# The inverse transform of a convolution in 32-column tiles, with the transpose on VectorE

## The chip, the cores and the metric

The kernel runs on one core of a Trainium2 chip. The metric is the device time in microseconds. Three runs of the kernel before gave 2071.14, 2072.65 and 2078.92 us; the median is 2072.65 us. All data is float32.

## The reference, cut to what matters

The program is a stack of two graph layers over 128 graphs of 128 nodes with 256 channels. The first layer normalizes x, and from the result h it makes a convolution over the nodes (1x1, then 17 taps, each with a batch norm), a message product over neighbours, and a gated update.

```
xc = transpose(h)                          # channels x nodes
c  = relu(bn1(conv1d(xc, conv1_w, 0)))
c  = bn2(conv1d(c, conv2_w, 8))            # 17 taps along the nodes
x_conv = transpose(relu(c + xc))
x_in = concat(x_conv, x_nmp)               # x_nmp: neighbours' messages
gi = x_in @ w_ih.T + b_ih ;  gh = h @ w_hh.T + b_hh
r = sigmoid(gi_r + gh_r) ;  z = sigmoid(gi_z + gh_z)
n = tanh(gi_n + r * gh_n)
x = x + (1 - z) * n + z * h
```

The second layer takes the first 25 nodes of each graph through five small graph convolutions and adds the result to x.

## The kernel before, in words

**The 17-tap convolution as products at frequencies.** The kernel doesn't run 17 products per node. It cuts the 128 nodes of a graph into two blocks of 64 outputs, each of which needs 80 inputs, and transforms these into F = 80 real frequency values. Stage A (`stage_a`) normalizes x, makes the 1x1 convolution and transforms into X. Stage B (`stage_b`) multiplies X by the transformed weights, frequency by frequency, and stores the result in DRAM as yd, with one 80x256 plane (frequency by channel) per block. Stage C (`stage_c`) reads four such planes at a time as the tile yt, transforms back with the constant matrix inv (80 frequencies by 64 nodes), and makes the gated update. A stage works on groups q of four graphs, so there are 32 groups.

**The start of stage C** is what the change touches. For each half of a group (two graphs), L703 makes two matmuls: inv is the stationary operand, with 64 columns, and the planes of block 0 or 1 of the two graphs are the moving operand, with 2 x 256 columns. They land in partitions 0 to 63 and 64 to 127 of the PSUM tile pi, so that pi holds nodes on partitions and channels along the free axis. ScalarE copies pi to xi in SBUF (L705). The rest of stage C wants channels on partitions. So the function turn_back (L710 to L724) transposes xi on TensorE, in blocks of 128x128, into the PSUM tile pc (L717); VectorE multiplies by the batch norm's scale and adds hT (the normalized input, channels on partitions), which gives xc (L720), and ScalarE adds the shift and applies Relu (L723). xc has two channel chunks (`xc[:, 0]` and `xc[:, 1]`) and two halves of columns.

**The gates** follow as products of weights with hT, xm (the neighbours' messages) and xc. They are made with a fast 2x2 scheme of seven products. For i below 3, product i takes a quarter of x as it stands; the others take one of four differences, which are made ahead on VectorE and are called th, tm and tc for the three inputs (`sums`, L586):

```
def factor(i, x, t):
    return ((x[:, 0, :D], x[:, 1, :D], x[:, 1, D:])[i] if i < 3
            else t[:, (3, 0, 1, 2)[i - 3]])
```

Products 0, 5 and 4 begin with the terms of hT and xm alone (the loop at L765, four matmuls each), and turn_back stands after the first of them. Then come the xc term of product 0 (L771), the sums tc (L773 to L775), three products of the hidden weights (L787 to L790, with VectorE's additions L791 and L792 behind them), all of product 1 (L794) and the xc terms of products 5 and 4, which read tc (L797, L802). At the end of a group GpSimd makes the update from r and z in two times three operations (L864, L865, L867); the result is transposed on TensorE as po (L884) while the next group already runs.

**What sets the order.** The kernel writes the order of its instructions by hand: each stage is a generator that issues some instructions and yields two numbers, the time that they are thought to take on TensorE and a pause. The class Order picks, by these numbers and by weights, which lane goes on. During stage C the lanes are the loads, stage C itself, the remaining message products (`early`), the normalization for the second layer (`rows`) and the second layer (`prepare`, `block`). Every engine then takes its instructions strictly in that order. PSUM tiles with the tag tmp rotate through five banks (`ptmp`), those with the tag gat through three (`pgat`). In SBUF, xi and tc share one buffer (tag tc), and xc has one buffer.

Of the kernel before, what the change touches and what calls it, by code (L numbers as in the profile page):

```python
# [9 lines left out]
FP = mybir.dt.float32  # L10
AF = mybir.ActivationFunctionType
ALU = mybir.AluOpType
# [3 lines left out]
B, N, D = 128, 128, 256  # L16
# [3 lines left out]
P = 128  # L20
GB = 4
NQ = B // GB

F = 80
# [17 lines left out]
WIDE = 32  # L42
# [165 lines left out]
def kernel(ctx: ExitStack, tc: tile.TileContext, x, adj, consts, vecs, w_se, conv1_w,  # L208
                    conv2_w, w_msg, b_msg, w_ih, w_hh, W1, W2, b2, fusion_w, out):
    nc = tc.nc  # L210
# [7 lines left out]
    ptmp = ctx.enter_context(tc.tile_pool(name="ptmp", bufs=5, space=PSUM))  # L218
# [14 lines left out]
    def c(name):  # L233
        a, b = CAT[name]
        return cst[:, a:b]
# [5 lines left out]
    ident = c("ident")  # L241
    fwd, inv = c("fwd"), c("inv")
# [15 lines left out]
    scl, sft = {}, {}  # L258
# [341 lines left out]
    def load_yt(q, h):  # L600

        if q < NQ:
            IN2[q, h] = LATE["co"].tile([F, GB, D], FP, tag="yt", name=f"yt{q}_{h}", bufs=2)
            x0 = (q % BQ * 2 + h) * GB
            nc.sync.dma_start(out=IN2[q, h],
                              in_=yd[q // BQ][x0:x0 + GB].rearrange("x f c -> f x c"))
# [80 lines left out]
    def stage_c(q):  # L687
# [7 lines left out]
            load_yt(q, 1)  # L695
            yield 0.0, 6.0
        fr = LATE["co"]
        xi = fr.tile([P, GB, D], FP, tag="tc", name=f"xi{q}")
        for h in range(2):
            yt = IN2.pop((q, h))  # L700
            pi = ptmp.tile([P, 2, D], FP, tag="tmp", name=f"pi{q}_{h}")
            for b in range(2):
                nc.tensor.matmul(pi[b * 64:(b + 1) * 64], inv[:F], yt[:, b::2],  # L703
                                 start=True, stop=True)
            nc.scalar.activation(xi[:, 2 * h:2 * h + 2], pi, AF.Copy)  # L705
            load_yt(q + 1, h)
            yield 0.86, 0.0
        xc = fr.tile([P, 2, 512], FP, tag="xc", name=f"xc{q}")

        def turn_back():  # L710

            for h in range(2):
                s = slice(h * D, (h + 1) * D)
                pc = ptmp.tile([P, 2, D], FP, tag="tmp", name=f"pc{q}_{h}")
                for co in range(2):
                    for i in range(2):
                        nc.tensor.transpose(pc[:, co, i * P:(i + 1) * P],  # L717
                                            xi[:, 2 * h + i, co * P:(co + 1) * P], ident)
                for co in range(2):
                    nc.vector.scalar_tensor_tensor(xc[:, co, s], pc[:, co],  # L720
                                                   scl["bn2"][:, co:co + 1], hT[:, co, s],
                                                   op0=ALU.mult, op1=ALU.add)
                    nc.scalar.activation(xc[:, co, s], xc[:, co, s], AF.Relu,  # L723
                                         bias=sft["bn2"][:, co:co + 1])  # L724

        wrz, wn, wh = LATE["wrz"], LATE["wn"], LATE["wh"]

# [5 lines left out]
        def part(ps, w, i, xs, first, last, again=False):  # L733


            n = [(m, o) for o in xs for m in range(w.shape[3] // P)]
            for j, (m, (k, x, t)) in enumerate(n):
                nc.tensor.matmul(ps[:, m], w[:, i, k, m * P:(m + 1) * P], factor(i, x, t),  # L738
                                 start=first and j == 0, stop=last and j == len(n) - 1,
                                 skip_group_check=again)  # L740
# [24 lines left out]
        for ps, i in ((p1, 0), (p6, 5), (p5, 4)):  # L765
            part(ps, wrz, i, early, True, False)
            yield 1.75, 0.0
            if i == 0:
                turn_back()
                yield 0.9, 0.0  # L770
        part(p1, wrz, 0, xs[2:], False, True)  # L771
        nc.scalar.activation(u2, p1, AF.Copy)  # L772
        tcs, todo = sums("tc", q, xc)  # L773
# [351 lines left out]
    for bat, (during_a, during_b) in enumerate(((0.66, 0.5), (0.2, 0.65))):  # L1125
# [12 lines left out]
        tc.tile_pool(name="co", bufs=1, side="right", reuse_waits="tile"))  # L1138
    loads = Lane([stage_n(q) for q in range(NQ)])
    groups = Lane([stage_c(q) for q in range(NQ)], ahead=2)  # L1140
    second = [setup_1()] + [part(blk) for blk in range(NBLK) for part in (prepare, block)]
    beside.weight = 0.5
# [43 lines left out]
```

## Time and profile before

| | |
|---|---|
| Median of three runs | 2072.65 us |
| Profiled execution, span of the core | 2070.6 us |
| TensorE busy | 2032.3 us (98%) |
| VectorE busy | 1161.9 us (56%) |
| ScalarE busy | 712.7 us (34%) |
| GpSimd busy | 730.1 us (35%) |
| mean granted TensorE clock | 0.993 |
| inverse transforms (L703) | 64 halves, first at 681.4 us, last at 1946.7 us |

PE is TensorE, PEld its weight loads, DVE VectorE, ACT ScalarE, POOL GpSimd, SP SyncE. The profile is of one execution; its span runs from the first to the last instruction. A matmul appears as two records and a transpose on TensorE as one. "L720" is line 720 of the kernel. In a row of the groups, "out<-in" names the tiles written and read, then come the shapes, the count, the busy time in us, the mean length of one in ns, and the time for which the engine was idle just before, with what ended it. The chain of work that ended last is followed back from the last instruction; on it, each piece begins when the one before it lets it begin. Lengths of neighbouring TensorE records overlap, because matmuls are pipelined; so the pace is read from the starts, or from the chain.

### The profile page before, as it was taken

How to read it: one execution, taken by the hardware profiler on the slowest of the kernel's cores; microseconds unless marked ns; L12 is line 12 of the kernel's file. 1: busy time of each engine (PE TensorE's matmuls, PEld its weight loads, DVE VectorE, ACT ScalarE, POOL GpSimd, SP SyncE). 2: the span in 40 equal slices, each digit the busy share in tenths (PEclk: the TensorE clock that was granted, in tenths of full speed). 3: DMA queues.
4: the chain of work that ended last, by engine and by line, in shares of the span. 5: the costliest groups of instructions: out<-in, count | busy, mean ns of one | idle time of the engine just before them, and what ended most of it. 6: DMA issues, size and time to landing. Idle time of an engine off the chain costs nothing.

```text
span 2070.6 us, 31082 instructions
## 1 busy us (share of the span) xinstructions
PE 2032.3 (98%) x11316; PEld 1649.4 (80%) x11316; DVE 1161.9 (56%) x2711; ACT 712.7 (34%) x1611; POOL 730.1 (35%) x898
## 2 busy tenths in 40 slices
PE   7998999999999999999999999999999999999998
PEld 5667888888888788788778787878787888778875
DVE  6774445874433556646654654566456655654542
ACT  4663223444222444233222332232332323323333
POOL 3552665333664123322422243233223323233230
PEclk9999999999999999899999999999999999999999
DMA  9997788545777444223323232322232332323121
GB/s 215 294 284 237 259 273 269 180 153 202 254 257 249 142 125 139 75 75 90 85 62 90 84 83 76 106 79 75 82 93 72 81 96 80 86 77 102 35 74 52
DMA packets 190135, 281.72 MB, mean 136 GB/s; under 512 B 23625, under 2 KB 143374, under 8 KB 189982
## 3 DMA queue, kind: packets, MB, share of 16 engines
q1 hardware_dynamic: 156942, 185.46, 31.4%
q0 software_dynamic: 32656, 93.98, 14.3%
q8 instruction: 90, 1.47, 0.3%
q14 instruction: 63, 0.52, 0.1%
q10 hardware_dynamic: 384, 0.28, 0.1%
HBM read 187.34 MB, written 92.27 MB: 135 GB/s over the span
## 4 chain that ended last, share of the span: by engine, by line
PE 93%; DVE 2%; DMA 2%; POOL 1%; issue 1%; ACT 1%; SPq 0%; DVEq 0%; POOLq 0%; ACTq 0%
PE p L738 42%; PE pa L526 7%; PE pm L630 5%; PE ph L1044 5%; PE pz L1053 5%; PE pc L421 4%; PE pb L526 3%; PE pi L703 3%; PE pf L432 3%; PE px L656 3%; PE pg L1087 2%; PE po L884 1%; PE pc L717 1%; PE pw L474 1%; PE ph L410 1%; PE py L1027 1%
## 5 line engine op out<-in xcount | busy, mean ns | idle before, releaser
L864 POOL TENSOR_TENSOR d<-hTc,r 128x512 f32<-128x512 f32 x64 | 81.9, 1280 | 244.4 <-ACT r L861 233.8
L526 PE MATMUL pa<-wf,X 128*128 128x256 f32 x640 | 152.2, 381 | 0.0
L893 POOL DMA_DIRECT2D out<-xt x128 | 72.0, 569 | 214.5 <-DVE xt L890 211.6
L558 DVE SCALAR_TENSOR_TENSOR y<-pa,kk 128x512 f32<-128x512 f32 x78 | 53.8, 690 | 151.2 <-ACT kk L557 151.1
L753 ACT ACTIVATE z<-z,brz 128x256 f32<-128x256 f32 x128 | 58.1, 501 | 226.7 <-DVE z L810 192.9
L738 PE MATMUL p<-th,wrz 128*128 128x256 f32 x512 | 132.8, 382 | 0.0
L738 PE MATMUL p<-tm,wrz 128*128 128x256 f32 x512 | 132.3, 381 | 0.0
L738 PE MATMUL p<-tc,wrz 128*128 128x256 f32 x512 | 131.5, 379 | 0.0
L526 PEld LDWEIGHTS pa<-wf,X 128*128 128x128 f32 x640 | 118.1, 190 | 16.2 <-issue 2.0
L630 PE MATMUL pm<-wmsg,hT 128*128 128x256 f32 x512 | 123.5, 387 | 0.0
L421 PE MATMUL pc<-c1w,hTa 128*128 128x256 f32 x512 | 121.6, 384 | 1.2 <-ACT hTa L412 1.2
L720 DVE SCALAR_TENSOR_TENSOR xc<-pc,s_bn,hTc 128x256 f32<-128x256 f32 x128 | 53.1, 478 | 123.3 <-PE pc L717 123.3
L1046 ACT ACTIVATE hh<-ph,vec 128x96 f32<-128x96 f32 (+3 forms) x160 | 64.2, 402 | 136.6 <-PE ph L1044 127.0
L630 PEld LDWEIGHTS pm<-wmsg,hT 128*128 128x128 f32 x512 | 97.1, 193 | 16.0 <-ACT kk L557 1.4
L1044 PE MATMUL ph<-yz,w 128*128 128x96 f32 (+3 forms) x640 | 108.4, 322 | 1.0 <-issue 1.0
L421 PEld LDWEIGHTS pc<-c1w,hTa 128*128 128x128 f32 x512 | 94.5, 191 | 18.3 <-DVE h L424 4.8
L738 PEld LDWEIGHTS p<-tm,wrz 128*128 128x128 f32 x512 | 97.9, 191 | 13.5
L1053 PE MATMUL pz<-hh,w 128*128 128x96 f32 (+3 forms) x640 | 107.3, 321 | 0.0
L738 PEld LDWEIGHTS p<-th,wrz 128*128 128x128 f32 x512 | 94.9, 191 | 13.0 <-issue 0.8
L738 PEld LDWEIGHTS p<-tc,wrz 128*128 128x128 f32 x512 | 95.0, 190 | 12.1 <-issue 0.5
L738 PE MATMUL p<-hTc,wrz 128*128 128x256 f32 x384 | 102.9, 391 | 1.6 <-ACT u L772 1.6
L1044 PEld LDWEIGHTS ph<-yz,w 128*128 128x128 f32 x640 | 86.7, 190 | 21.0 <-issue 15.4
(202 smaller groups left out, 4557.1 us busy)
## 6 DMA issues: line engine op xcount, KB each, us to landing
wf<-wfd SPq DMA_DIRECT2D x160, 256.0 KB, 3.5
wfd<-ws POOLq DMA_DIRECT2D x64, 320.0 KB, 9.2
yd<-y POOLq DMA_DIRECT2D x80, 256.0 KB, 4.3
yt<-yd SPq DMA_DIRECT2D x64, 320.0 KB, 5.0
w<-in_W SPq DMA_DIRECT2D x40, 512.0 KB, 3.6
xa<-in_x SPq DMA_DIRECT2D x128, 128.0 KB, 5.5
hTd<-hTa POOLq DMA_DIRECT2D x32, 512.0 KB, 6.6
hT<-hTd SPq DMA_DIRECT2D x32, 512.0 KB, 6.2
```

What stands on the lines that cost most here:

```text
L421: nc.tensor.matmul(pc[:, i], hT[:, k, (2 * h + i) * N:(2 * h + i + 1) * N], c1w[:, k], start=(k == 0), stop=(k == 1))
L432: nc.tensor.matmul(pf[:, i, :F * NB], h1[:, 2 * h + i, k * P:(k + 1) * P], fwd, start=True, stop=True)
L526: nc.tensor.matmul(ps, xk(k), WF[f][:, k, s], start=(k == 0), stop=(k == 1))
L630: nc.tensor.matmul(pm[:, i], hT[:, k, j * N:(j + 1) * N], LATE["wmsg"][:, k], start=(k == 0), stop=(k == 1))
L656: nc.tensor.matmul(px[:, dc, i], msgs[h][:, i, dc * P:(dc + 1) * P], aT[:, 2 * h + i], start=True, stop=True)
L703: nc.tensor.matmul(pi[b * 64:(b + 1) * 64], inv[:F], yt[:, b::2], start=True, stop=True)
L738: nc.tensor.matmul(ps[:, m], w[:, i, k, m * P:(m + 1) * P], factor(i, x, t), start=first and j == 0, stop=last and j == len(n) - 1, skip_g ...
L864: nc.gpsimd.tensor_sub(d, hT[:, dc], r[:, dc])
L893: nc.gpsimd.dma_start(out=out[q * GB + j, WIDE:].rearrange("(t n) c -> n t c", n=WIDE), in_=xt[j * WIDE:(j + 1) * WIDE, 1:4])
L1044: nc.tensor.matmul(ph, w1[:, k, m * P:(m + 1) * P], yz[:, k, :, o:o + n], start=(k == 0), stop=(k == 1))
L1046: nc.scalar.activation(hh[:, m], ph, AF.Relu, bias=v("b1", g * 4 + m))
L1053: nc.tensor.matmul(pz, w2[:, g, m, cc * P:(cc + 1) * P], hs[g][:, m], start=(m == 0), stop=(m == 3))
```

## The change

The inverse transform swaps nothing between stationary and moving, but cuts both finer. For each half group there are four blocks n of 32 nodes (two blocks of 64, each in two) and four slices w of 32 channels in each of the two chunks of 128. A matmul now has 32 columns of inv as the stationary operand, and slice w of both chunks and both graphs as the moving operand, 2 x 2 x 32 = 128 columns. It writes partitions 32w to 32w + 31 of pi, so that a quadrant of partitions stands for one channel slice, and a run of 32 values along the free axis is the slice's channels. VectorE's transpose of 32x32 blocks then turns each block on its way from PSUM to xi, which leaves channels on partitions and nodes along the free axis. The transposes on TensorE, the tile pc and the ScalarE copy are gone, and so is the step turn_back: the scale, the addition of hT and Relu follow each half's transpose at once, with xi in SBUF as input. Both halves are now one step of the generator, without a pause between them.

```diff
-        xi = fr.tile([P, GB, D], FP, tag="tc", name=f"xi{q}")
+        xi = fr.tile([P, 2, 512], FP, tag="tc", name=f"xi{q}")
+        xc = fr.tile([P, 2, 512], FP, tag="xc", name=f"xc{q}")
         for h in range(2):
             yt = IN2.pop((q, h))
-            pi = ptmp.tile([P, 2, D], FP, tag="tmp", name=f"pi{q}_{h}")
-            for b in range(2):
-                nc.tensor.matmul(pi[b * 64:(b + 1) * 64], inv[:F], yt[:, b::2],
-                                 start=True, stop=True)
-            nc.scalar.activation(xi[:, 2 * h:2 * h + 2], pi, AF.Copy)
+            pi = ptmp.tile([P, 2, 2, 4, WIDE], FP, tag="tmp", name=f"pi{q}_{h}")
+            for n in range(4):
+                o = n % 2 * WIDE
+                for w in range(4):
+                    nc.tensor.matmul(
+                        pi[w * WIDE:(w + 1) * WIDE, :, :, n].rearrange("p k g c -> p g k c"),
+                        inv[:F, o:o + WIDE],
+                        yt[:, n // 2::2].rearrange("f g (k w c) -> w f g k c", k=2, w=4)[w],
+                        start=True, stop=True)
+            nc.vector.transpose(xi[:, :, h * D:(h + 1) * D],
+                                pi.rearrange("p k g n c -> p k (g n c)"))
             load_yt(q + 1, h)
-            yield 0.86, 0.0
-        xc = fr.tile([P, 2, 512], FP, tag="xc", name=f"xc{q}")
-
-        def turn_back():
-
-            for h in range(2):
-                s = slice(h * D, (h + 1) * D)
-                pc = ptmp.tile([P, 2, D], FP, tag="tmp", name=f"pc{q}_{h}")
-                for co in range(2):
-                    for i in range(2):
-                        nc.tensor.transpose(pc[:, co, i * P:(i + 1) * P],
-                                            xi[:, 2 * h + i, co * P:(co + 1) * P], ident)
-                for co in range(2):
-                    nc.vector.scalar_tensor_tensor(xc[:, co, s], pc[:, co],
-                                                   scl["bn2"][:, co:co + 1], hT[:, co, s],
-                                                   op0=ALU.mult, op1=ALU.add)
-                    nc.scalar.activation(xc[:, co, s], xc[:, co, s], AF.Relu,
-                                         bias=sft["bn2"][:, co:co + 1])
+            s = slice(h * D, (h + 1) * D)
+            for co in range(2):
+                nc.vector.scalar_tensor_tensor(xc[:, co, s], xi[:, co, s],
+                                               scl["bn2"][:, co:co + 1], hT[:, co, s],
+                                               op0=ALU.mult, op1=ALU.add)
+                nc.scalar.activation(xc[:, co, s], xc[:, co, s], AF.Relu,
+                                     bias=sft["bn2"][:, co:co + 1])
+        yield 1.8, 0.0
...
         for ps, i in ((p1, 0), (p6, 5), (p5, 4)):
             part(ps, wrz, i, early, True, False)
             yield 1.75, 0.0
-            if i == 0:
-                turn_back()
-                yield 0.9, 0.0
```

## The prediction

> **What bounds the kernel now.** I began with the busy shares, the slices and the chain of work that ended last.
>
> ```profile
> PE 2032.3 (98%) x11316; PEld 1649.4 (80%) x11316; DVE 1161.9 (56%) x2711; ACT 712.7 (34%) x1611; POOL 730.1 (35%) x898
> ...
> PE   7998999999999999999999999999999999999998
> ...
> PE 93%; DVE 2%; DMA 2%; POOL 1%; issue 1%; ACT 1%; SPq 0%; DVEq 0%; POOLq 0%; ACTq 0%
> ```
>
> TensorE is the bound: 93% of the chain is its own work. The table by stretches sharpens this for the time in which stage C runs: TensorE is idle 3.8 us of the 230 us from 680 to 910 us, and 2.9 us of the 1147 us from 910 to 2057 us. What leaves TensorE there leaves the span, unless somebody is then late. Next, one group of stage C (32 such groups run) on the chain in order of time; columns are start, length, work.
>
> ```profile
> 1317.55 1.87 PE pi L703 x8
> 1319.42 1.92 PE p L738 x8
> 1321.34 0.87 PE pc L717 x8
> 1322.21 8.21 PE p L738 x38
> 1330.42 0.87 PE po L884 x8
> ```
>
> Without a gap, the inverse transform takes 1.87 us and the transposes back 0.87 us. A written matmul leaves two records, a transpose one. The nearest relative of the new matmuls is the product pse, also with 32 stationary columns per tile, four output quadrants and 128 moving columns:
>
> ```profile
> 709.24 0.57 PE pse L614 x16
> ```
>
> Its sixteen records take 0.57 us; the eight records of pc, also of 128 columns but one at a time, take 0.87 us (0.109 each). One at a time sixteen would need 1.74 us. So four tiles do run side by side: four slots of 0.109 us and 0.13 us for going in and out. The old pi fits the same reading with two tiles side by side: 512 columns are four times 0.109, so four slots are 1.74 us, and 0.13 us makes 1.87.
>
> VectorE gets the rest of the change. These are rows of its groups by form (count, then busy us and mean ns, then idle before):
>
> ```profile
> L720 DVE SCALAR_TENSOR_TENSOR xc<-pc,s_bn,hTc 128x256 f32<-128x256 f32 x128 | 53.1, 478 | 123.3 <-PE pc L717 123.3
> L658 DVE COPY xnmp<-px 128x512 f32<-128x512 f32 x64 | 43.5, 685 | 11.4 <-PE px L656 11.3
> ```
>
> and this the timeline of a group whose pi starts at 1550.03 us (call that T), with only VectorE's and GpSimd's rows kept:
>
> ```profile
> 1550.56 1.27 POOL L864 TENSOR_TENSOR d<-hTc,r 128x512 f32<-128x512 f32 x1 [13.37 <-ACT r L861]
> ...
> 1554.37 1.66 DVE L720 SCALAR_TENSOR_TENSOR xc<-pc,s_bn,hTc 128x256 f32<-128x256 f32 x4 [3.81 <-PE pc L717]
> ...
> 1557.19 1.33 POOL L867 TENSOR_TENSOR z<-d,r 128x512 f32<-128x512 f32 x1
> 1557.49 1.30 DVE L586 TENSOR_TENSOR tc<-xc,tc 128x256 f32<-128x256 f32 x1
> 1558.72 0.41 DVE L586 TENSOR_TENSOR tc<-xc 128x256 f32<-128x256 f32 x1
> ```
>
> The previous group's six GpSimd operations run from T+0.5 to T+8.5. A VectorE operation with both inputs in SBUF takes 1.30 us beside one of them and 0.41 us after the last. L720, with one input in PSUM, runs at its normal pace beside them.
>
> **What the Trainium skill says.** "TensorE: Matmul & The Clock Gate", Part 3, says that outputs in different 32-partition quadrants make matmuls run concurrently; pse agrees (0.57 against 1.74 us). "PSUM — Partial Sum Buffer", Specifications, warns that a non-contiguous pattern slows matmuls. The new output is four runs of 32 values per tile, and no matmul before writes such a pattern; short runs in the moving operand are shown harmless by L1044, which reads 144 columns in runs of 9 values: sixteen records from 1456.38 to 1458.34 us, 0.122 each, just 0.109 scaled by the columns. "SBUF — State Buffer", SBUF: two separate sides, calls the port pair of VectorE and GpSimd an exclusive lock that a VectorE operation with two SBUF inputs needs; 1.30 against 0.41 us agrees. "Vector Engine (DVE) Microarchitecture Reference", 3.8, says that the 32x32 transpose sustains one element per cycle per lane; no transpose ran on VectorE before.
>
> **The change, part by part.**
>
> *Removed from TensorE*: eight transposes per group, 0.87 us, 32 times: 27.8 us.
>
> *Changed on TensorE*: four matmuls of 64x512 become 32 of 32x128. Per half group there are four node blocks n with four channel slices w each, w innermost, so each four neighbours go to four quadrants. That is 64 records, 16 slots of four: 16 x 0.109 + 0.13 = 1.87 us, as before. The pse records start 0.110 apart, so I add 0.02 us: 1.89. Weight loads are as narrow as those of pse and already paid in its slot. Unknown is whether the pace holds beyond sixteen records. At best it is 1.87. The skill's price for the start-to-start floor of short matmuls (same TensorE page, Part 1) is about 25 ns; 64 of these would be 1.6 us (estimate), so it would not bind. At worst only two of the four run together, 32 slots: 3.6 us. I take 1.89.
>
> *Removed from ScalarE*: 64 copies of 0.587 us (37.6 us). Worth nothing: ScalarE is 34% busy, and only turn_back waited for them.
>
> *Added to VectorE*: 64 transposes of 128x512 out of PSUM. Nearest row: the copy L658, 0.685 us. Below: one element per cycle, 512 at the 0.96 GHz that the skill gives, 0.53 us (estimate); above: four times the copy, 2.7 us. I take 0.7: 45 us in all, VectorE from 56% to 58%.
>
> *Moved on VectorE*: the four L720 operations now read xi from SBUF, so both inputs are there: 0.41 us alone, about 1.3 us beside GpSimd, and they now come when GpSimd is active. So I walk the queue. The old ScalarE copy started 1.2 us after T, when the first half lay ready: transpose 0 runs T+1.2 to 1.9. The two operations of that half each wait for a GpSimd operation to end: done T+3.4 and 4.8. Transpose 1, which needs only one port: 5.5. Then T+6.0 and 7.4, with ScalarE's Relu (0.5) after each. The sums tc follow at T+8.7 to 9.8. Consumers: the first matmul on xc came at 1558.06, T+8.03; without pc and with 0.02 more it comes at T+7.2. It reads only half 0, chunk 0 (factor 0), ready at T+3.9: 3.3 us to spare. The first matmul on tc (factor 5, t[:, 1]) came 5.6 us later, so now T+12.8; its sum is ready at about T+9.1: 3.7 us to spare. If the cover were gone, VectorE's stretch from transpose 0 to the last Relu would be on the path, 6.7 us per group.
>
> Behind these on VectorE stand the additions L791 and L792, which began at T+10.1 before and can begin at T+9.8 now. GpSimd loses at most four times 0.3 us and the output transposes po, at T+12 now, still come after its end at about T+9.7.
>
> *Buffers and order.* xi lies in the single tc buffer and xc in its single buffer; the last matmuls that read their old contents stand ahead of pi on TensorE, so neither adds a wait. pi 1's bank stays taken until T+5.5 instead of T+2.6; of the five, the next product to reuse it is po. In the built order nothing but the twelve early matmuls stands between pi and the first xc product in 27 of the 32 groups; elsewhere more work does, which only adds cover. The yt loads still wait on pi, at the same distance. Removing the pauses lets other lanes fall differently in groups 2 to 6; with 3.8 us of idle time there, I allow 4 us either way.
>
> *Sum*: 32 x (0.87 - 0.02) = 27.2 us. The profiled span is 2070.6 us, so 2043.4; the median of the runs, 2072.65, lies 2 us above the span, so about 2046 us, 1.3% faster.
>
> **Rivals.**
>
> *The four tiles don't keep step (slower).* Place: the 64 records of pi. Either the strided output or the density halves the pace to two tiles at a time: 3.6 instead of 1.89 us, 32 x (0.85 - 1.73) = -28, so 2101 us. For it: nowhere before do more than sixteen such records follow each other, and the densest 10 us hold 89 matmul records, 112 ns each against the 28 ns needed. Against it: that stretch is full of wide weight loads, and nothing in pse slows towards its end. It decides where pi takes over 2.74 us, 43 ns per record.
>
> *VectorE becomes late.* The walk above with transposes of 2.7 us gives xc at T+5.2 and tc at about T+10.4, still in time; with 5 us each, tc is ready at T+15.4, which costs 2.6 us per group: 2046 + 83 = 2129 us. Break-even is at about 4.5 us per transpose, over six times the copy of the same size; hence unlikely. In a mild form, waits in the mixed stretch before 910 us, where five groups carry 1.4 us more VectorE work, give at most 7 us: 2053.
>
> *No difference that can be told.* If pi takes 2.5 us because the strided output costs a third more per slot, 32 x (0.87 - 0.63) = 8 us: 2065 us.
>
> **How the numbers follow.** I give the plain gain 0.70 (2040 to 2054), a part of it lost in slots or mixed stretches, but still faster by over 0.5%, 0.08 (2054 to 2062), the loss of nearly all 0.08 (2062 to 2083), two tiles at a time 0.11, VectorE late 0.03. Half a per cent, 10.4 us, is about what a measurement of this kernel tells from nothing; so faster 0.78, same 0.08, slower 0.14. The lower end, 2039, is the plain sum with pi unchanged and 4 us of idle time gained; the upper end, 2072, takes in the lost gain and leaves about 0.18 outside.
>
> **What will show it.** On the chain, pi at 1.9 us with 64 records and no pc between the early products; the table by stretches with TensorE still idle only a few us after 910; the transpose's row at 0.6 to 0.8 us; the L720 operations at around 1.3 us beside GpSimd and no TensorE wait on xc, tc or the Relu. I am wrong if the pi records start over 0.11 us apart in groups of four or in pairs, or if VectorE appears as TensorE's releaser in each group.

## The result and the profile after

The changed kernel takes 2049.99 us (median of four runs, 2048.49 to 2053.76); the kernel before, run beside it, 2073.2 us (2071.14 to 2078.92). The ratio is 0.988, with a 95% interval of 0.986 to 0.9901: about 23 us less, where 27 were predicted. The forecast of 2046 us was 4 us too low. The profiled execution took 2049.36 us, its span is 2047.5 us.

The page of the kernel after, with its busy shares, TensorE's busy tenths in the 40 slices, and the chain that ended last:

```profile
PE 2006.3 (98%) x12852; PEld 1659.2 (81%) x12852; DVE 1285.1 (63%) x2775; ACT 688.5 (34%) x1547; POOL 741.3 (36%) x898
...
PE   7998999999999999999999999999999999999998
...
PE 89%; DVE 3%; issue 3%; POOL 3%; DMA 2%; ACT 1%; SPq 0%; POOLq 0%; DVEq 0%; ACTq 0%
```

TensorE is still the bound, but its share of the chain fell from 93% to 89%, and GpSimd's rose from 1% to 3%. That is the first hint of where the missing microseconds are. VectorE is at 63%, not at the 58% that was forecast for it.

The chain of the kernel after over a group early in stage C (start, length, work):

```profile
1304.16 1.88 PE pi L706 x64
1306.05 10.13 PE p L735 x46
1316.17 0.87 PE po L878 x8
```

The 64 records of the new inverse transform take 1.88 us, the transposes pc are gone, and the gate products run through. (The lines moved with the change: L703 is now L706, L720 is L716, L738 is L735, L772 is L766, L864 to L867 are L858 to L861.)

VectorE's and GpSimd's groups by form, after (count, then busy us and mean ns, then idle before):

```profile
L716 DVE SCALAR_TENSOR_TENSOR xc<-xi,s_bn,hTc 128x256 f32<-128x256 f32 x128 | 148.1, 1195 | 2.3
L711 DVE STREAM_TRANSPOSE xi<-pi 128x512 f32<-128x512 f32 x64 | 45.4, 709 | 17.8 <-PE pi L706 17.8
L858 POOL TENSOR_TENSOR d<-hTc,r 128x512 f32<-128x512 f32 x64 | 87.2, 1362 | 299.3 <-ACT r L855 288.7
```

The transpose of 32x32 blocks takes 0.709 us for 128x512 values. The operation with two SBUF inputs went from 478 to 1195 ns, and since the profile counts the longer time as busy, it alone adds 95 us to VectorE's busy time (148.1 less 53.1). GpSimd's own operation d became longer too, from 1280 to 1362 ns on average.

**Where the rest of the gain went.** Stage C, from the first pi to the end of the span, takes 2047.5 - 679.5 = 1368.0 us, against 2070.6 - 681.4 = 1389.2 us before. That is 21.2 us instead of 27.2. The 680 us ahead of it, whose instructions are the same in both, differ by 1.9 us. To find the place, here is the timeline of the group whose pi starts at T = 1338.50 us, one that the second layer doesn't interrupt (start, length, engine, line, work, and in brackets the idle time before it with what ended it):

```profile
1339.65 0.72 DVE L711 STREAM_TRANSPOSE xi<-pi 128x512 f32<-128x512 f32 x1 [0.62 <-PE pi L706]
1340.40 2.23 DVE L716 SCALAR_TENSOR_TENSOR xc<-xi,s_bn,hTc 128x256 f32<-128x256 f32 x2
...
1345.48 0.51 ACT L719 ACTIVATE xc<-xc,t_bn 128x256 f32<-128x256 f32 x1 [0.90 <-DVE xc L716]
...
1346.66 1.32 POOL L861 TENSOR_TENSOR z<-d,r 128x512 f32<-128x512 f32 x1
...
1348.01 0.60 ACT L766 ACTIVATE u<-p 128x512 f32<-128x512 f32 x1 [2.02 <-PE p L735]
...
1348.66 1.13 PE L735 MATMUL p<-hTc,wrz 128*128 128x256 f32 x4 [0.67 <-ACT u L766]
```

The last row is TensorE waiting: 0.67 us, for ScalarE's copy u (L766). This is the copy of product 0 to the tile u2, which must be taken before product 1 accumulates onto the same bank. The copy began at 1348.01, just after GpSimd's last operation L861 ended at 1347.98. (The bracket of the copy names TensorE, because another product, L735, ended at about the same time. Product 0 itself had ended at 1346.70, and in 17 other groups the profile names GpSimd.) The code says why (comments added):

```
u2 = fr.tile([P, 2, D], FP, tag="u2", name=f"u2{q}")            # this group's copy of product 0
d  = fr.tile([P, 512], FP, tag=f"u{2 + dc}", name=f"d{q}_{dc}")   # GpSimd's update, dc = 1, then 0
```

The d of dc = 0 lies in the buffer of u2, and GpSimd reads it last, in the L861 that closes the previous group's update. So the copy of the new group must wait for the whole of GpSimd's update of the old one. The view of the tile u confirms it, after:

```profile
its engine sat idle before it (us, times) until:
  PE p L735: 105.6, 82
  POOL z L861: 17.5, 17
who waited for it (us, times):
...
  PEld p L735: 12.0, 18
  PE p L735: 4.9, 7
```

And before:

```profile
  POOL z L867: 4.8, 1
who waited for it (us, times):
...
  PE p L738: 1.6, 1
```

Idle time of TensorE understates the delay, so it is also counted group by group. Where nothing waits, the first matmul that reads tc comes 12.79 us after T. Of the 26 groups after 910 us, 25 have no other lane's work in between; in 16 of these the matmul comes later, by 7.3 us in sum. In the kernel before, the one wait delayed it by 1.9 us. The net loss to u2 is 5.4 us. One more wait for the copy, of 1.8 us, stands in group 4 (counted from 0), before 910 us. It is of another kind: ScalarE was busy with the second layer right up to the copy.

The table by stretches shows the granted clock as a further effect (columns: busy us and count for TensorE, its weight loads, VectorE, ScalarE, GpSimd, then granted TensorE clock, DMA share, GB/s). Before:

```profile
840.00:870.00 30.00, 26.80 (x109) 19.42 (x108) 16.00 (x42) 6.49 (x14) 15.01 (x21) 0.77 0.16 46
```

And after:

```profile
840.00:870.00 30.00, 28.22 (x136) 23.76 (x133) 24.21 (x57) 7.82 (x19) 15.90 (x24) 0.94 0.29 67
910.00:2030.00 1120.00, 1114.95 (x7135) 918.77 (x7134) 736.28 (x1519) 328.30 (x713) 345.68 (x392) 1.00 0.30 82
```

Before, a wait of 2.5 us from 843.8 us came with matmuls at half pace, and these 30 us ran at a granted clock of 0.77; after, at 0.94. That is worth about 30 x (0.94 - 0.77) = 5 us. It comes with a wait for VectorE that the new order doesn't have at this place, and not with the transform itself.

After 910 us the clock reads 1.00, but that is a rounded mean over 1120 us. Short windows find two places in the kernel after where TensorE was busy throughout and ran at about half the clock:

```profile
1254.00:1258.00 4.00, 4.00 (x17) 3.55 (x17) 2.86 (x8) 0.57 (x2) 2.15 (x3) 0.57 0.00 0
1452.00:1456.00 4.00, 4.00 (x18) 3.73 (x19) 1.56 (x6) 0.71 (x3) 2.07 (x3) 0.57 0.00 0
```

Each loses 4 x (1 - 0.57) = 1.7 us, 3.4 us together. The kernel before has no such drop between 910 us and its last group. TensorE is idle 5.05 us from 910 to 2030 us instead of 2.7, and 4.5 us instead of 3.8 in the first six groups. The sum is then 27.2 - 5.4 (u2) + 5 (clock before 910 us) - 3.4 (the two drops) - 0.7 (idle in the first groups) = 22.7 us, against 21.2 measured; 1.5 us stay unassigned.

### The profile page after: what moved, and what is told of

Read it like the earlier page. It is cut to its first block, busy times and chain, and to the rows that moved or that the text cites. A ratio compares the mean times of both kernels' runs of the same rounds, so it can differ in the third digit from the quotient of the medians.

```text
span 2047.5 us, 34132 instructions
## 1 busy us (share of the span) xinstructions
PE 2006.3 (98%) x12852; PEld 1659.2 (81%) x12852; DVE 1285.1 (63%) x2775; ACT 688.5 (34%) x1547; POOL 741.3 (36%) x898
## 4 chain that ended last, share of the span: by engine, by line
PE 89%; DVE 3%; issue 3%; POOL 3%; DMA 2%; ACT 1%; SPq 0%; POOLq 0%; DVEq 0%; ACTq 0%
PE p L735 39%; PE pa L526 7%; PE pm L630 5%; PE ph L1038 5%; PE pz L1047 5%; PE pc L421 4%; PE pb L526 3%; PE pf L432 3%; PE px L656 3%; PE pi L706 3%; PE pg L1081 1%; PE pw L474 1%; PE po L878 1%; PE ph L410 1%; PE py L1021 1%
## 5 line engine op out<-in xcount | busy, mean ns | idle before, releaser
L858 POOL TENSOR_TENSOR d<-hTc,r 128x512 f32<-128x512 f32 x64 | 87.2, 1362 | 299.3 <-ACT r L855 288.7
L716 DVE SCALAR_TENSOR_TENSOR xc<-xi,s_bn,hTc 128x256 f32<-128x256 f32 x128 | 148.1, 1195 | 2.3
L735 PE MATMUL p<-tm,wrz 128*128 128x256 f32 x512 | 132.3, 381 | 0.0
L735 PE MATMUL p<-th,wrz 128*128 128x256 f32 x512 | 132.1, 380 | 0.0
L735 PE MATMUL p<-tc,wrz 128*128 128x256 f32 x512 | 131.8, 380 | 0.0
L719 ACT ACTIVATE xc<-xc,t_bn 128x256 f32<-128x256 f32 x128 | 64.8, 508 | 138.8 <-DVE xc L716 138.8
L735 PEld LDWEIGHTS p<-tm,wrz 128*128 128x128 f32 x512 | 97.8, 191 | 13.5
L735 PE MATMUL p<-hTc,wrz 128*128 128x256 f32 x384 | 103.9, 393 | 5.0 <-ACT u L766 4.9
L735 PEld LDWEIGHTS p<-th,wrz 128*128 128x128 f32 x512 | 97.1, 190 | 13.6 <-PE p L735 0.2
```

The source lines that it names most:

```text
L716: nc.vector.scalar_tensor_tensor(xc[:, co, s], xi[:, co, s], scl["bn2"][:, co:co + 1], hT[:, co, s], op0=ALU.mult, op1=ALU.add)
L719: nc.scalar.activation(xc[:, co, s], xc[:, co, s], AF.Relu, bias=sft["bn2"][:, co:co + 1])
L858: nc.gpsimd.tensor_sub(d, hT[:, dc], r[:, dc])
```

## The experiments

Theory A: the missing gain is the wait for u2, and it comes from the buffer that u2 shares with GpSimd's d. Theory B: the wait is ScalarE's queue, in which the Relu of the second half stands ahead of the copy. A further question was why pi keeps its pace, and how much margin VectorE has.

**The changed kernel again.** No edit; it runs beside those that follow.

> The changed kernel once more, so that the next two can be set beside it on the same chip. Both theories: about 2050 us, some 23 us under the kernel before, and again waits of TensorE for the ScalarE copy u2 in about half of the groups, 7 to 9 us in sum.

It took 2052.76 us (2050.47 to 2055.72), ratio 0.9898 (0.988 to 0.9915). Stage C takes 1366.2 us. The u2 waits are there again: 7.24 us in 16 of 25 groups.

**Let GpSimd's tiles change places.** The d that GpSimd finishes first now takes u2's buffer:

```diff
-            d = fr.tile([P, 512], FP, tag=f"u{2 + dc}", name=f"d{q}_{dc}")
+            d = fr.tile([P, 512], FP, tag=f"u{3 - dc}", name=f"d{q}_{dc}")
```

> GpSimd's two update tiles d change places: the one that is finished last takes u3's buffer, the first one u2's. Theory A, that TensorE waits for the ScalarE copy u2 because u2 shares its buffer with the tile d that GpSimd finishes last in the group before: the waits on u2 vanish, 7 to 9 us less than the changed kernel, about 2042 us. Theory B, that the copy is held by the Relu operations ahead of it in ScalarE's queue: no difference, about 2050 us.

It took 2045.94 us (2042.46 to 2051.09), ratio 0.9866 (0.9845 to 0.9887), 6.8 us below the run of the changed kernel beside it. The intervals of the two ratios just overlap, so the trace has to carry the verdict. The tile u in this kernel:

```profile
its engine sat idle before it (us, times) until:
  PE p L735: 110.4, 90
who waited for it (us, times):
...
  PEld p L735: 2.6, 2
  PE p L735: 1.8, 1
```

GpSimd is gone as a releaser. The one wait of 1.8 us that is left is that of group 4, behind ScalarE's own work. None of the 25 groups has a wait for u2. In the group that matches the one shown above, with T = 1344.40 us, the copy now starts while GpSimd's L861 still runs:

```profile
1352.56 1.33 POOL L861 TENSOR_TENSOR z<-d,r 128x512 f32<-128x512 f32 x1
1352.69 0.60 ACT L766 ACTIVATE u<-p 128x512 f32<-128x512 f32 x1 [0.79 <-PE p L735]
```

Stage C takes 1360.7 us, 5.5 less than the changed kernel beside it. Theory A holds. Against the kernel before beside it, the medians now differ by 28.4 us.

**Issue the second half's Relu after the copy u2**, with the buffers as in the changed kernel:

```diff
-                nc.scalar.activation(xc[:, co, s], xc[:, co, s], AF.Relu,
-                                     bias=sft["bn2"][:, co:co + 1])
+                if h == 0:
+                    nc.scalar.activation(xc[:, co, s], ...)
...
         nc.scalar.activation(u2, p1, AF.Copy)
+        for co in range(2):
+            nc.scalar.activation(xc[:, co, D:], ...)
```

> The Relu of the second half of xc is issued on ScalarE behind the copy u2 instead of ahead of it. Theory A (shared buffer): no gain, about 2050 us, the waits on u2 stay. Theory B (ScalarE's queue): the waits go, about 2042 us.

It took 2050.37 us (2046.97 to 2053.01), ratio 0.989 (0.9873 to 0.9907). The tile u here:

```profile
  POOL z L865: 69.9, 18
who waited for it (us, times):
...
  PEld p L736: 11.6, 18
  PE p L736: 4.6, 7
```

ScalarE reaches the copy earlier and then sits idle 69.9 us for GpSimd instead of 17.5; TensorE's waits stay, 6.87 us in 16 of 25 groups. So B is refuted as the cause in the changed kernel.

**The exchange of buffers in the kernel before.** The same one-line edit, without the change under study:

> The exchange of the two d buffers alone, on the kernel before. If the wait on u2's buffer was made by the change, there is next to nothing to gain here: TensorE lost 1.8 us to u2 in the whole profile before, so 2071 to 2073 us. If the buffer had held the kernel before as well, it gains the 7 us that it gained on the changed kernel, about 2066 us.

It took 2076.1 us (2072.85 to 2082.55, 14 runs), ratio 1.0007 (0.9994 to 1.002). No gain shows in the time. In the trace GpSimd is gone as a releaser of u here too, and with it the kernel's one wait of 1.9 us, which is too little to see in the time. In every other undisturbed group the kernel before had room: the copy was due at T+9.15 us, and GpSimd ended at T+6.5 to 8.9. The change brought the copy forward to T+8.29 and GpSimd's end back, to as late as T+9.5.

**Take away the contention, not the shared buffer.** VectorE's transpose writes a PSUM tile, and L716 has one input in PSUM, as before the change:

```diff
-            nc.vector.transpose(xi[:, :, h * D:(h + 1) * D],
-                                pi.rearrange("p k g n c -> p k (g n c)"))
+            xp = ptmp.tile([P, 2, D], FP, tag="tmp", name=f"xp{q}_{h}")
+            nc.vector.transpose(xp, pi.rearrange("p k g n c -> p k (g n c)"))
...
-                nc.vector.scalar_tensor_tensor(xc[:, co, s], xi[:, co, s],
+                nc.vector.scalar_tensor_tensor(xc[:, co, s], xp[:, co],
```

> VectorE's transpose writes to a PSUM bank instead of SBUF, so that the scale-and-add has one input in PSUM again; the d buffers stay as in the changed kernel. If the two-SBUF-input form is what makes these operations slow beside GpSimd, their mean falls from 1195 to about 480 ns and GpSimd's L858 from 1362 to about 1280 ns. If the slower GpSimd is half of why u2's buffer comes late (0.5 us of it a group, the other 0.85 us being TensorE's earlier arrival), the waits on u2 fall from 7.2 us in 25 groups to 2 or 3, and the time to about 2047 us. If the earlier arrival alone does it, they stay at 6 to 7 us and the time near 2051 us.

Its groups by form:

```profile
L715 DVE SCALAR_TENSOR_TENSOR xc<-xp,s_bn,hTc 128x256 f32<-128x256 f32 x128 | 56.1, 480 | 2.3
L711 DVE STREAM_TRANSPOSE xp<-pi 128x512 f32<-128x512 f32 x64 | 46.5, 727 | 18.9 <-PE pi L705 18.8
L857 POOL TENSOR_TENSOR d<-hTc,r 128x512 f32<-128x512 f32 x64 | 82.6, 1290 | 298.1 <-ACT r L854 287.5 <-issue 10.5
```

With one input in PSUM the operation is back at 480 ns and GpSimd's d at 1290. The u2 waits fall to 3.84 us in 8 of 25 groups, between the two expectations. About half of the new wait goes with GpSimd's delay by contention, and what is left with TensorE's earlier arrival. The time, 2049.7 us (2046.86 to 2054.93), ratio 0.9877 (0.9859 to 0.9896), does not tell this from the changed kernel; only the trace does.

**Both together**, the exchange of buffers and the transpose into PSUM:

> Both: the exchanged d buffers and the transpose into PSUM. With no wait on u2 left, a faster VectorE and GpSimd stand beside the path: the same time as with the exchange alone, 2045 us, within 2 us. If VectorE's waits in the mixed stretch before 910 us count, up to 3 us less.

It took 2045.38 us (2041.69 to 2049.29), ratio 0.9854 (0.9833 to 0.9874), with no u2 wait after 910 us and a stage C of 1356.0 us. It has the lowest median, and its interval lies below that of the changed kernel's second run. Against the exchange alone the medians differ by only 0.6 us, which decides nothing. Stage C is 4.7 us shorter in the trace: TensorE is idle 3.4 us instead of 4.5 in the first six groups, where VectorE's waits count a little, and the granted clock dropped once instead of three times (3.4 us at half each, so 3.4 us in all).

**Quadrant in the outer loop.** The same 64 matmuls per group, but each quadrant's four follow each other:

```diff
-            for n in range(4):
-                o = n % 2 * WIDE
-                for w in range(4):
+            for w in range(4):
+                for n in range(4):
+                    o = n % 2 * WIDE
```

> The two loops of the inverse transform are exchanged, so that four matmuls in a row go to the same quadrant and only then to the next. If only neighbours in the queue run side by side, the 64 records take 0.109 us each, 7.1 instead of 1.88 us a group, and the kernel about 2050 + 32 x 5.2 = 2217 us. If TensorE finds free tiles further down its queue, pi stays near 1.9 us and the kernel near 2050 us.

A single run took 2119.02 us, with a stage C of 1432.8 us. On the chain:

```profile
1412.49 4.26 PE pi L706 x64
```

The result lies between both expectations. With eight records in a row per quadrant, side-by-side work shrinks but does not end. It fits a quadrant that starts when four of the eight records before it have started: eight runs of eight make 7 x 4 x 0.109 + 8 x 0.109 + 0.13 = 4.05 us (an estimate), against 4.26; one after the other they would need 64 x 0.109 = 7.0. The kernel also has no wait for u2, since TensorE asks for the copy 2.4 us later.

**Two matmuls in a row per quadrant**, four records, is the step between:

```diff
-            for n in range(4):
-                o = n % 2 * WIDE
-                for w in range(4):
+            for n0 in range(0, 4, 2):
+                for w, n in [(w, n) for w in range(4) for n in (n0, n0 + 1)]:
+                    o = n % 2 * WIDE
```

> Two matmuls in a row per quadrant (four records), then the next quadrant. With eight records in a row per quadrant a group's pi took 4.26 us, each quadrant overlapping with the last four records of the one before. If what counts is that a quadrant may begin once at most four records of the one before are open, four in a row let all quadrants run together, and pi is 1.9 to 2.3 us, the kernel 2050 to 2063 us. If overlap is only ever between two neighbours in the queue, pi is near 3.6 us and the kernel near 2100 us.

```profile
1303.53 1.95 PE pi L706 x64
```

The chain gives pi 1.95 us, and a single run 2049.04 us. Runs of four records per quadrant cost 0.07 us, runs of eight 2.4 us. So "four records still to start" fits both kernels, and "half of the run before" does not: for runs of four it would give 15 x 2 x 0.109 + 4 x 0.109 + 0.13 = 3.84 us. Why it is four is not shown.

**VectorE's margin: each transpose twice.** With the buffers exchanged, so that GpSimd stays out of it; the second transpose repeats the first, hence 0.7 us more per half:

```diff
-            nc.vector.transpose(xi[:, :, h * D:(h + 1) * D],
-                                pi.rearrange("p k g n c -> p k (g n c)"))
+            for _ in range(2):
+                nc.vector.transpose(xi[:, :, h * D:(h + 1) * D],
+                                    pi.rearrange("p k g n c -> p k (g n c)"))
```

> With the exchanged d buffers, each transpose on VectorE is made twice (1.4 us more VectorE work a group, the same result). By the walk through VectorE's queue there are about 3 us to spare for xc and tc in the groups after 910 us: no wait there, and 0 to 7 us more in the mixed stretch, so 2045 to 2052 us. If VectorE is on the path, 32 x 1.4 = 45 us more, 2090 us.

It took 2067.79 us (2065.03 to 2071.01), ratio 0.996 (0.9948 to 0.9973). Stage C is 1379.0 us, 18.3 more than with single transposes. Neither side had expected that. The timeline of the group with T = 1583.94 us:

```profile
1592.97 0.51 ACT L720 ACTIVATE xc<-xc,t_bn 128x256 f32<-128x256 f32 x1 [0.91 <-DVE xc L717]
...
1593.39 0.58 ACT L767 ACTIVATE u<-p 128x512 f32<-128x512 f32 x1
...
1594.02 1.13 PE L736 MATMUL p<-hTc,wrz 128*128 128x256 f32 x4 [0.58 <-ACT u L767]
```

TensorE waits for u2 once more, but the copy now stands behind the last Relu in ScalarE's queue, and that Relu waits for VectorE. The matmuls wait in 18 of 25 groups, and no wait is on xc or tc. So theory B, wrong for the changed kernel, names the next limit behind it. The waits for u2 sum to 16.3 us by the count of the groups, most of the 18.3. The first six groups lose as well. Here are their windows with single transposes, and with double ones (the first two numbers behind the window are its length and TensorE's busy time):

```profile
688.60:953.60 265.00, 260.46 (x1743) 219.47 (x1744) 173.10 (x375) 93.59 (x199) 71.54 (x88) 0.99 0.37 106
687.00:955.70 268.70, 260.74 (x1739) 219.31 (x1738) 179.77 (x387) 93.06 (x198) 71.78 (x88) 0.99 0.37 105
```

TensorE is idle 8.0 us there instead of 4.5.

**Transposes twice, and the second half's Relu after the copy.** The edits of the last kernel and of the third one together:

> The doubled transposes with the exchanged d buffers, and the Relu of the second half issued behind the copy u2. In the run before TensorE waited for u2 (some 15 us in the groups after 910 us) and never for xc or tc. Theory: u2 stands in ScalarE's queue behind the last Relu, which waits for VectorE, and this is the next limit once the buffer is free. Then the waits go and the time is about 2048 us. Rival: VectorE itself is late for the products; then TensorE waits for xc or tc instead, and the time stays at 2060 us or more.

It took 2051.74 us (2046.94 to 2057.95), ratio 0.989 (0.9862 to 0.9918). No group after 910 us waits for u2, xc or tc. With this order VectorE can be 1.4 us later per group there without a wait; the 16 us of waits belonged to the place of a Relu in a queue. Stage C, at 1367.7 us, is still 7.0 us longer than with single transposes, all of it in the first six groups: TensorE is idle 8.3 us there instead of 4.5, and two more drops of the clock cost 3.4 us. So where the lanes mix, the doubled transposes do reach TensorE.

**All three edits**, exchange, PSUM and late Relu, with single transposes:

> All three together: exchanged d buffers, transpose into PSUM, Relu of the second half behind u2. No wait on u2 was left with the first two, so nothing is expected of the third: 2045 us, within 2 us of the run with the first two.

It took 2052.68 us (2044.11 to 2055.57), ratio 0.9879 (0.9857 to 0.9901): a miss by its median. Stage C is 1363.5 us, 7.5 longer than without the late Relu. The loss comes in steps: 2.7 us by group 6, then some 1.7 us each near groups 9, 14 and 29. None is a wait for u2, which neither kernel has after 910 us; from group 9 to the last TensorE is not idle at all in either. The granted clock is what differs. In this profile it drops five times before the last group, each time to half for 3.4 us, at 909, 1035, 1264, 1653 and 1848 us. Without the late Relu it drops once, at 1644 us. One of the five:

```profile
1264.10:1267.50 3.40, 3.40 (x18) 3.40 (x17) 1.61 (x5) 1.06 (x4) 2.06 (x3) 0.51 0.00 0
```

Four more drops make 4 x 1.7 = 6.8 of the 7.5 us. The runs agree: this kernel takes 2049.16 us at a mean clock of 0.992 and 2044.11 us at 0.994, the one without the late Relu 2049.29 us at 0.992 and 2045.26 and 2045.50 us at 0.994. At the same clock no cost of the third edit shows. Why the clock dropped more often, and whether the edit has a part in it, stays open.

## Why the prediction was right, and where it was off

- **pi keeps its pace: right.** 1.88 us against 1.89. The strided output and the 64 records in a row cost nothing that shows; the slowing by non-contiguous patterns of which the prediction quotes a warning did not appear. The rival of two tiles at a time (3.6 us) is out by the chain, and the rival with a third more per slot (2.5 us) too.
- **pc removed: right.** The first xc matmul comes at T+7.17 us, predicted T+7.2.
- **The transpose on VectorE: right.** 0.709 us against 0.7. VectorE late as a rival is out for the groups after 910 us: with twice the transposes nothing waited for xc or tc there. But where the working named only these consumers, the doubled transposes found another through ScalarE's queue. The rival's mild form, waits in the mixed stretch, was real for doubled transposes (3.4 us more idle time); for the change itself it is at most some 1 us.
- **L720 with two SBUF inputs beside GpSimd: the duration was right** (about 1.3 us estimated there, 1195 ns on average), its consequence was not. VectorE's share was forecast at 58% and is 63%: the sum counted the transposes and left out the longer operations, though the walk had their length. VectorE's share had no part in the time by itself. That a second SBUF input is the condition is shown by the kernel that has one input in PSUM: 480 ns.
- **"Buffers and order": this step failed.** It asked of xi and xc whether their buffers add a wait, and of ptmp's banks, and stopped there. The copy u2 was not on the list, though it is the next thing that TensorE needs from ScalarE after the first xc product. It shares its buffer with GpSimd's d. The working had the delay: it put GpSimd's end at about T+9.7, and T+9.48 was measured in the group shown. But it judged it against po alone, at T+12. The copy was due at T+8.3, and these two numbers were never set side by side. The runs: 7.3 us of waits in 16 of 25 groups, none with the buffers exchanged, half with the contention taken away, and no such gain by the exchange in the kernel before.
- **The sum: 27.2 us, measured 21.2 in stage C and 23.2 in the medians.** The terms themselves were right: pi at 1.88 us and pc's 0.87 us gone are read from the chain, and without the u2 wait the medians differ by 28.4 us. The missing term is this wait, 5.4 us net. But there is luck in how near the forecast came: the clock gave some 5 us before 910 us and took 3.4 us after it in the profile, and the prediction had neither.
- **The mixed stretch before 910 us** was allowed 4 us either way, for idle time. TensorE's idle time in the first six groups rose by only 0.7 us; the gain of about 5 us there is clock.
- **Small slips in the sums.** The rival of two tiles at a time counts 0.02 us per group twice, which makes 0.6 us. The lower end of the range, 2039 us, is worked out from the profiled span; from the median it would be 2041. VectorE with 45 us more on the shorter span makes 59%, not 58%. The price of 25 ns between starts, which the prediction uses only to show that it would not bind, does not hold between quadrants: the four records of a slot start 6 to 7 ns apart. None of these changes a verdict.

## What to carry to other kernels

When work leaves the engine that sets the end, list everything that this engine will now ask for sooner, including the buffers that other engines' tiles share by name, and walk each back to its last reader. A delay that contention brings to a second engine is to be held against all of that engine's consumers, not only the one that comes first to mind. For matmuls in quadrants, put the quadrant in the innermost loop. And before a few microseconds are put down to the order of instructions, look at the granted clock in short windows: a mean that reads 1.00 can hide several drops.

## What the runs showed of the hardware that was not expected

- The side-by-side work of quadrants depends on the order of issue: 64 records take 1.88 us with the quadrant innermost, 1.95 us with four records in a row per quadrant, 4.26 us with eight.
- VectorE's transpose of 32x32 float32 blocks out of PSUM is about as fast as a copy: 709 ns into SBUF and 727 ns into PSUM for 128x512, against 685 ns for the copy L658.
- The granted clock dropped to half for 3.4 us at a time, 1.7 us lost each, also where TensorE had no idle time (0.51 from 1264.1 to 1267.5 us in the kernel with all three edits). The number of drops differs between two profiles of the same kernel: after the start of group 9, two in one profile of the changed kernel and one in the other.
- One PSUM input in place of an SBUF one took a VectorE operation beside a busy GpSimd from 1195 to 480 ns.
- The start of stage C lay between 679.4 and 690.3 us in these profiles, though the instructions ahead of it are the same. About half of this is clock: ahead of the earliest start it stood at half for 6.8 us in all, ahead of the latest for 17.1, so 3.4 against 8.5 us were lost. A single profile's span is therefore a poor judge of a few microseconds; the length of stage C is a better one once its clock drops are counted, and the waits in it are better still.
